# A graph network on one core: choosing the path without GpSimd, and three chunks gathered ahead

## The chip, the core and the metric

The kernel runs on one core of one Trainium2 chip. A core has a matrix engine (TensorE, PE in the profile, with its weight loads as PEld), VectorE (DVE), ScalarE (ACT), GpSimd (POOL) and SyncE (SP); all but VectorE and TensorE also issue transfers here, GpSimd the indirect ones that gather rows by an index. The metric is the time of one execution on the device, in microseconds; lower is better.

## The reference

A graph has N = 6250 nodes with 160 features each and E = 200,000 edges. Edges are sorted by destination. Two layers follow each other; each ends in a residual sum and a layer norm:

```python
# layer 0, per edge e: features of the source, weighted by the edge's four attributes
ss, vv = s[src], v[src]
m = concatenate([C0 * (ss*e0 @ W1 + dot(vv, e1)*INV3 @ W2), C1 * (p3 + p4 + p5)])
h = segment_sum(m, dst, num_segments=N) @ (Ws, Wv)
x1 = layernorm(2*x + relu(h))
# layer 1: an edge network gives weights w0..w3 of the messages
w = (relu(edge_attr_10 @ W_fc1) @ W_fc2)          # split into w0, w1, w2, w3
y = linear(x1)[src]                               # gathered by source again
out = layernorm(x1 + linear_si(x1) + 0.5 * o(segment_sums of w*y*e, dst))
```

What costs time is that 200,000 rows are gathered by `src` and summed by `dst`, in each of the two layers.

## The kernel before

Edges are cut into NCH = 391 chunks of 512: four edges on each of the 128 partitions. The host only lays arrays out: `src` and `dst` come as 128 x 391 x 4 integers. Since edges are sorted, the destinations of one chunk lie close together. For a chunk the kernel makes a one-hot matrix of (destination minus lowest destination of the chunk), at most 32 wide, scales it by the four edge attributes (`onehot`), and sums with it on TensorE (`matmuls`, L427); the result is transposed on VectorE (L447, L444) and added at a dynamic offset `low` to the accumulator `acc` (`add`, L449). The last 79 chunks (from HALF = 312) are treated as two half chunks, "windows", of 64 partitions each, so that there are NWIN = 470 windows.

This works only while no chunk spreads further than its width and no destination lies below what is closed already. So the kernel starts with a choice of path, in `gnn_kernel`: it computes the lowest and highest destination of every window, compares them with the constants `wide` and `closed`, and puts 1 or 0 into `fits`. Every engine loads `fits` and branches: `windowed` is the fast path, which runs here; `general` is the other one, which is never entered with these inputs.

The order in the choice of path before: constants by memsets on VectorE (L143); `src` on ScalarE's queue and `dst` on SP's; GpSimd makes `iota` (L154) and the identity matrix, then gathers chunk 0 (`gathered`, L206: four indirect transfers of 128 rows of 640 bytes). VectorE converts the destinations to floats (L159, `rel`), reduces over the four edges of each partition (L166, L167). GpSimd's all-reduce (L170) takes the maximum over partitions; the lowest enters it negated. Then GpSimd gathers chunk 1. VectorE evaluates the test on one partition (L175 to L190), and subtracts each window's lowest destination from `rel` (L193).

In `windowed`, VectorE first sets `eps` and `zero` (L229, L231). ScalarE clears `acc` with `zero` as its input (`clear`, L241, five pieces). The function `sums` issues the stages of a layer by hand, in steps t: `load` of chunk t, `onehot` of t-1, `matmuls` of t-2 and `add` of t-3 in layer 0; layer 1 adds `hidden` (L394, L397) and `message` (L407 to L415). Chunks 0 and 1 are in the tile `early`, the others go through a ring of GRING = 8 buffers `g`. At step 8 `prepare` builds the weights `wb` and `wn` of layer 0's end and `wc` of layer 1. When a block of 128 nodes is complete it goes through `projected` (with `wb`, L461), a layer norm, `linear` (with `wn`, L525), and is written to the table `ytab` from which layer 1 gathers.

In layer 1 the ten attributes of four chunks are loaded at a time into a tile `et` (L342). Two such tiles alternate: one is the memory of `early`, the other is a tile of its own from a pool `xp`. The order of the instructions on each engine is the order of the program here (`manual_schedule`), but for transfers, which the planner may put ahead on their queue.

Of the kernel before, what the change touches and what calls it, by code (L numbers as in the profile page):

```python
# [22 lines left out]
M0, M1 = 64, 32  # L23
J = 4
CH = P * J
NCH = -(-E // CH)
# [12 lines left out]
W = 32  # L39
NW = N + W + 2  # L40
HALF = 312
NWIN = HALF + 2 * (NCH - HALF)
WIDTHS = ((3, 32), (128, 16), (208, 24), (HALF, 32), (NCH, 24))
GRING = 8
PREPARE = 8


def expected(node, sign):
# [30 lines left out]
POS = {c: i for i, c in enumerate(ORDER)}  # L79
# [32 lines left out]
@with_exitstack  # L112
def gnn_kernel(ctx: ExitStack, tc: tile.TileContext, x, src, dst, ea, sh, avec,
               w1t, w2t, w3t, w4t, w5t, ws, wv, wsi0, wsi1, wl10, wl11,
               w00, w10, w01, w11, wfc1, wfc2, out):

    nc = tc.nc
    weights = (w1t, w2t, w3t, w4t, w5t, ws, wv, wsi0, wsi1, wl10, wl11, w00, w10, w01, w11, wfc1, wfc2)
    keep = ctx.enter_context(tc.tile_pool(name="keep", bufs=1))
    rel = keep.tile([P, NCH, J], F32, name="rel")
    srcs = keep.tile([P, NCH, J], I32, name="srcs")
    low = keep.tile([1, NWIN + 1], I32, name="low")  # L130
    fits = keep.tile([1, 1], I32, name="fits")
    ident = keep.tile([P, P], F32, name="ident")
    iota = keep.tile([P, W], F32, name="iota")
    early = keep.tile([P, 2, J, D], F32, name="early")
    ahead = {}
    with tc.manual_schedule(), tc.tile_pool(name="ends", bufs=1) as ep:
        dsts = ep.tile([P, NCH, J], I32, name="dsts")
        closed = ep.tile([1, NWIN], F32, name="closed")
        wide = ep.tile([1, NWIN], F32, name="wide")

        def fill(row, chunk, end, value):
            if chunk < end:
                nc.vector.memset(row[:, windows(chunk)[0]:windows(end - 1)[-1] + 1], float(value))  # L143

        begin = 0
        for c in range(1, NCH + 1):
            if c == NCH or floor_of(c) != floor_of(begin):
                fill(closed, begin, c, floor_of(begin))
                begin = c
        for (end, w), begin in zip(WIDTHS, (0,) + tuple(e for e, _ in WIDTHS)):  # L150
            fill(wide, begin, end, w)
        nc.scalar.dma_start(srcs, src)
        nc.sync.dma_start(dsts, dst)
        nc.gpsimd.iota(iota, pattern=[[1, W]], base=0, channel_multiplier=0,  # L154
                       allow_small_or_imprecise_dtypes=True)
        make_identity(nc, ident)

        ahead[0] = gathered(nc, early[:, 0], srcs, x, 0)
        nc.vector.tensor_copy(rel, dsts)  # L159

        mm = ep.tile([P, 2, NWIN], F32, name="mm")
        halves = [(slice(64 * h, 64 * h + 64), slice(HALF + h, NWIN, 2), slice(HALF, NCH)) for h in range(2)]
        parts = [(slice(0, P), slice(0, HALF), slice(0, HALF))] + halves
        nc.vector.memset(mm[:, :, HALF:NWIN], -2.0 * N)
        for rows, wins, chunks in parts:
            nc.vector.tensor_reduce(mm[rows, 0, wins], rel[rows, chunks, :], AX.X, ALU.max)  # L166
            nc.vector.tensor_reduce(mm[rows, 1, wins], rel[rows, chunks, :], AX.X, ALU.min)  # L167
            nc.vector.tensor_scalar(mm[rows, 1, wins], mm[rows, 1, wins], -1.0, None, op0=ALU.mult)
        mx = ep.tile([P, 2, NWIN], F32, name="mx")
        nc.gpsimd.partition_all_reduce(mx.rearrange("p a c -> p (a c)"), mm.rearrange("p a c -> p (a c)"),  # L170
                                       P, bass_isa.ReduceOp.max)
        ahead[1] = gathered(nc, early[:, 1], srcs, x, 1)
        nc.vector.memset(low, 0)
        lowf = ep.tile([1, NWIN], F32, name="lowf")
        nc.vector.tensor_scalar(lowf, mx[0:1, 1, :], -1.0, 0.0, op0=ALU.mult, op1=ALU.max)  # L175
        nc.vector.tensor_scalar(low[:, 0:NWIN], lowf, float(N), None, op0=ALU.min)
        far = ep.tile([1, 5], F32, name="far")
        span = ep.tile([1, NWIN], F32, name="span")
        nc.vector.tensor_add(span, mx[0:1, 0, :], mx[0:1, 1, :])
        nc.vector.tensor_sub(span, span, wide)  # L180
        nc.vector.tensor_reduce(far[:, 0:1], span, AX.X, ALU.max)
        for i, row in enumerate((mx[0:1, 0, 0:HALF], mx[0:1, 0, HALF:NWIN], mx[0:1, 1, :])):
            nc.vector.tensor_reduce(far[:, i + 1:i + 2], row, AX.X, ALU.max)
        nc.vector.tensor_add(closed, closed, mx[0:1, 1, :])
        nc.vector.tensor_reduce(far[:, 4:5], closed, AX.X, ALU.max)
        lim = ep.tile([1, 5], F32, name="lim")
        for i, v in enumerate((0, P * LATE, N + 1, 1, 1)):
            nc.vector.memset(lim[:, i:i + 1], float(v))
        nc.vector.tensor_tensor(far, far, lim, op=ALU.is_lt)
        nc.vector.tensor_reduce(fits, far, AX.X, ALU.min)  # L190
        for rows, wins, chunks in parts:
            n = chunks.stop - chunks.start
            nc.vector.tensor_tensor(rel[rows, chunks, :], rel[rows, chunks, :],  # L193
                                    mx[rows, 1, wins][:, :, None].to_broadcast([rows.stop - rows.start, n, J]),
                                    op=ALU.add)
    go = nc.values_load(fits[0:1, 0:1], min_val=0, max_val=1,
                        skip_runtime_bounds_check_because="a comparison's result")
    with tc.If(go > 0) as both:
        windowed(tc, x, srcs, rel, low, ident, iota, early, ahead, ea, sh, avec, *weights, out)
    with both.Else():  # L200
        general(tc, x, srcs, rel, dst, ea, sh, avec, *weights, out)


def gathered(nc, g, srcs, table, c):
    for j in range(J):
        nc.gpsimd.indirect_dma_start(out=g[:, j, :], out_offset=None, in_=table,  # L206
                                     in_offset=bass.IndirectOffsetOnAxis(ap=srcs[:, c, j:j + 1], axis=0))
    return g
# [3 lines left out]
def windowed(ctx: ExitStack, tc: tile.TileContext, x, srcs, rel, low, ident, iota, early, ahead, ea, sh, avec,  # L212
# [6 lines left out]
    nc = tc.nc  # L219
# [10 lines left out]
    zero = const.tile([P, 5], F32, name="zero")  # L230
    nc.vector.memset(zero, 0.0)  # L231
    a_sb = const.tile([P, NB], F32, name="a_sb")
    wb = const.tile([P, 5, D], F32, name="wb")
    wn = const.tile([P, 2 * D], F32, name="wn")
    wn2 = const.tile([M1, 2 * D], F32, name="wn2")
    wc = const.tile([P, 5, D], F32, name="wc")
    fc1 = const.tile([P, 100], F32, name="fc1")
# [74 lines left out]
    def sums(layer, table, gp, hp):  # L312
        with ExitStack() as s:
# [4 lines left out]
                up = s.enter_context(tc.tile_pool(name="up", bufs=1))  # L318
            pa = s.enter_context(tc.tile_pool(name=f"pa{layer}", bufs=3 if layer else 4, space=PSUM))
            if layer:  # L320
                xp = s.enter_context(tc.tile_pool(name="xp", bufs=1))
# [267 lines left out]
def general(ctx: ExitStack, tc: tile.TileContext, x, srcs, rel, dst, ea, sh, avec,  # L589
# [10 lines left out]
    nc = tc.nc  # L600
# [262 lines left out]
    with tc.tile_pool(name="any_acc0p", bufs=1) as ap0:  # L863
        acc = ap0.tile([P, NB, 4 * D], F32, name="acc0")
        sums(0, x, acc)
        with tc.tile_pool(name="any_n0", bufs=3) as np_, tc.tile_pool(name="any_n0t", bufs=1, space=PSUM) as pt, \
# [107 lines left out]
```

## Time and profile before

| what | value |
|---|---|
| median of three runs | 4930.06 us (4926.66 to 4936.89) |
| the profiled execution's own time | 4865.16 us |
| its span | 4863.0 us |
| PE, PEld busy | 2968.4 us (61%), 2222.4 us (46%) |
| DVE busy | 2162.4 us (44%) |
| ACT busy | 377.9 us (8%) |
| POOL busy | 2973.9 us (61%) |
| mean granted TensorE clock | 0.752 |
| layer 0, from the first ring gather to the last | 31.84 to 2248.4 us |
| first gather of layer 1 | 2291.78 us |

Times in the profile are microseconds from the start of the span. A row of the timeline gives start, duration, engine, line, operation, output and inputs, and in brackets how long the engine had been idle and what ended that. "remote" is an event that the profile can put down to no instruction of this core; "issue" is idle time in which the engine waited for nothing that the profile shows. A busy TensorE is not one at its peak, as its matmuls overlap and their ends are modelled.

### The profile page before, as it was taken

What the parts mean: (1) busy time and instruction counts of PE and PEld (TensorE: products, weight loads), DVE (VectorE), ACT (ScalarE), POOL (GpSimd) and SP (SyncE); (2) the same over time, 40 slices, a digit from 0 to 9 for tenths busy, and PEclk for the clock granted to TensorE, in tenths of its full rate; (3) what the DMA queues carried; (4) which work ended last, traced back from release to release, by engine and by line L of the source; (5) the groups of instructions that cost most, each with busy time, mean ns of one, the idle gap of its engine ahead of it and who ended that gap; (6) DMA issues with size and microseconds to landing.
All of it is one profiled execution on the core that took longest, in us unless ns stands there. A gap on an engine that the chain in (4) does not pass through costs nothing.

```text
span 4863.0 us, 42324 instructions
## 1 busy us (share of the span) xinstructions
PE 2968.4 (61%) x12714; PEld 2222.4 (46%) x12715; DVE 2162.4 (44%) x6948; ACT 377.9 (8%) x747; POOL 2973.9 (61%) x3137
## 2 busy tenths in 40 slices
PE   2333344444444444446587878777878788887777
PEld 1322333333333333434355555555555555555555
DVE  3222222232323333334355555555566566666656
ACT  2000000000000000001000000000100010101000
POOL 5666666666666666664665655565556656555553
PEclk7566655666666666667788888888888888888888
DMA  2222222222222222222222222222222222222221
GB/s 67 61 62 58 63 64 63 61 65 65 66 63 69 64 67 65 69 68 57 57 59 54 60 54 60 57 61 58 59 59 57 62 60 62 61 57 61 58 59 39
DMA packets 198246, 295.60 MB, mean 61 GB/s; under 512 B 59271, under 2 KB 140669, under 8 KB 198011
## 3 DMA queue, kind: packets, MB, share of 16 engines
q0 software_dynamic: 150144, 256.45, 21.4%
q1 hardware_dynamic: 40702, 31.55, 2.3%
q10 hardware_dynamic: 7164, 4.80, 0.3%
q8 instruction: 107, 1.75, 0.1%
q14 instruction: 129, 1.05, 0.1%
HBM read 280.57 MB, written 12.00 MB: 60 GB/s over the span
## 4 chain that ended last, share of the span: by engine, by line
PE 42%; another core or an unknown queue 33%; DVE 12%; issue 10%; POOL 2%; ACT 1%; DMA 0%; DVEq 0%; ACTq 0%; POOLq 0%
PE ab L427 24%; PE pw L407 11%; PE ph L394 3%; DVE m L415 3%; DVE S L385 2%; PE ph L461 2%; POOL g L206 2%; DVE acc L449 1%; PE bank L548 1%; DVE m L410 1%; DVE ab L444 1%; DVE ab L447 1%; DVE ab L445 1%; DVE bank L381 1%
## 5 line engine op out<-in xcount | busy, mean ns | idle before, releaser
L206 POOL DMA_INDIRECT g<-ytab,srcs x1564 | 1484.3, 949 | 1074.1 <-issue 438.5
L206 POOL DMA_INDIRECT g<-in_x,srcs x1556 | 1477.2, 949 | 741.8 <-issue 424.3
L427 PE MATMUL ab<-g,S 128*128 128x160 f32 (+1 forms) x3744 | 716.6, 392 | 818.6 <-issue 418.0
L427 PE MATMUL ab<-m,S 128*128 128x320 f32 (+1 forms) x3760 | 1087.9, 493 | 56.1 <-DVE acc L449 48.0
L427 PEld LDWEIGHTS ab<-g,S 128*128 128x128 f32 (+1 forms) x3744 | 638.5, 259 | 902.5 <-issue 441.2
L407 PE MATMUL pw<-fc,h 100*128 100x192 f32 x3128 | 737.3, 385 | 472.4 <-DVE m L415 375.1
L407 PEld LDWEIGHTS pw<-fc,h 100*128 100x128 f32 x3128 | 609.3, 222 | 703.1 <-issue 313.2
L427 PEld LDWEIGHTS ab<-m,S 128*128 128x128 f32 (+1 forms) x3760 | 698.3, 220 | 324.3 <-issue 161.9
L447 DVE STREAM_TRANSPOSE ab<-ab 128x160 f32<-128x160 f32 x470 | 169.6, 361 | 1232.0 <-remote 999.1
L385 DVE TENSOR_TENSOR S<-bank,sh 128x384 f32<-128x384 f32 (+2 forms) x782 | 431.5, 552 | 551.8 <-remote 189.8
L415 DVE TENSOR_TENSOR m<-g,pw 128x192 f32<-128x192 f32 x1564 | 475.9, 346 | 0.0
L410 DVE TENSOR_TENSOR m<-pw,g 128x256 f32<-128x256 f32 x782 | 328.1, 420 | 320.0 <-remote 208.9
L397 ACT ACTIVATE h<-ph 100x512 f32<-100x512 f32 x391 | 230.6, 597 | 2223.2 <-remote 983.1
L449 DVE TENSOR_TENSOR acc<-acc,ab 128x120 f32 (+2 forms) x940 | 261.7, 278 | 285.1 <-remote 176.3
L381 DVE TENSOR_TENSOR bank<-iota,rel 128x96 f32<-128x96 f32 (+2 forms) x782 | 200.2, 256 | 181.9 <-remote 96.9
L461 PE MATMUL ph<-wb,acc 128*128 128x160 f32 (+1 forms) x490 | 125.4, 430 | 246.9 <-DVE acc L449 107.2
L461 PEld LDWEIGHTS ph<-wb,acc 128*128 128x128 f32 (+1 forms) x490 | 109.6, 286 | 264.3 <-issue 117.1
L445 DVE STREAM_TRANSPOSE ab<-ab 32x160 f32<-32x160 f32 x470 | 165.5, 352 | 16.2
L444 DVE STREAM_TRANSPOSE ab<-ab 128x160 f32<-128x160 f32 x470 | 167.4, 356 | 10.7 <-issue 6.7
L394 PE MATMUL ph<-early,fc 10*100 10x512 f32 x392 | 114.9, 648 | 0.3
L394 PE MATMUL ph<-et,fc 10*100 10x512 f32 x390 | 112.0, 642 | 0.2 <-issue 0.2
L525 PE MATMUL pl<-wn,xT 128*128 128x320 f32 (+1 forms) x98 | 49.4, 593 | 87.1 <-issue 60.2
(80 smaller groups left out, 732.3 us busy)
## 6 DMA issues: line engine op xcount, KB each, us to landing
g<-ytab,srcs POOLq DMA_INDIRECT x1564
g<-in_x,srcs POOLq DMA_INDIRECT x1556
raw<-in_sh SPq DMA_DIRECT2D x88, 64.0 KB
early<-in_ea SPq DMA_DIRECT2D x98, 40.0 KB
xt<-in_x SPq DMA_DIRECT2D x48, 80.0 KB
ytab<-y ACTq DMA_DIRECT2D x48, 80.0 KB
btab<-base SPq DMA_DIRECT2D x48, 80.0 KB
et<-in_ea SPq DMA_DIRECT2D x96, 40.0 KB
```

What stands on the lines that cost most here:

```text
L206: nc.gpsimd.indirect_dma_start(out=g[:, j, :], out_offset=None, in_=table, in_offset=bass.IndirectOffsetOnAxis(ap=srcs[:, c, j:j + 1], axi ...
L381: nc.vector.tensor_tensor(oh[:, :, :w], iota[:, None, :w].to_broadcast([P, J, w]), rel[:, c, :, None].to_broadcast([P, J, w]), op=ALU.is_e ...
L385: nc.vector.tensor_tensor(S[c][:, :, :, :w], oh[:, :, None, :w].to_broadcast([P, J, 4, w]), attr[:, :, :, None].to_broadcast([P, J, 4, w]) ...
L394: nc.tensor.matmul(ph[:, i, :], fc1[g:g + 10, :], ET[c // 4][g:g + 10, c % 4 // 2, :], start=True, stop=True)
L397: nc.scalar.activation(H[c], H["p"][:, c % 2, :].rearrange("f (p j) -> f j p", j=J), AF.Relu, scale=FC_SCALE)
L407: nc.tensor.matmul(pw[:, j, :], h[:, q + j, :], fc2, start=True, stop=True)
L410: nc.vector.tensor_tensor(mq[:, :, :, 0:64], pw[:, :, 0:128].rearrange("p j (a u) -> p j a u", a=2), y[:, :, None, 0:64].to_broadcast([P, ...
L415: nc.vector.tensor_tensor(mq[:, :, a, 64:160].rearrange("p j (d u) -> p j d u", d=3), y1, pw[:, :, None, w:w + 32].to_broadcast([P, 2, 3, ...
L427: nc.tensor.matmul(ab[:, :n], one[h * i:h * i + h, j, :, :], t[h * i:h * i + h, j, :], start=(j == 0), stop=(j == J - 1), skip_group_check ...
L447: nc.vector.transpose(tr, blocks[:, 0])
L449: nc.vector.tensor_tensor(v, v, tr[:, :, :width(c)], op=ALU.add)
L461: nc.tensor.matmul(po[:r], lhs, weights[:, g, :], start=(g == 0), stop=(g == 4))
```

## The change

- `ramp`, 0 to 127 along each row, is made by VectorE with seven doublings, and `iota` becomes its first 32 columns. `ident` is a comparison of `ramp` with each partition's own number. GpSimd makes neither.
- The indices of the first three chunks come in a small transfer of their own, `first`; all three chunks are gathered into `early`, which grows from two chunks to three, ahead of the choice. `dst` goes to ScalarE's queue, `src` to SP's behind `first`.
- `wide` and `closed` are brought onto partitions, one window per row and five columns ("folds": three of 104 chunks, and the two halves of the last 79), by ten matmuls with a one.
- Highest and lowest of each partition are reduced over all 391 chunks, transposed on TensorE (four transpositions each), and reduced along the row on VectorE. The all-reduce goes.
- The test works on 104 partitions and five columns; failures are counted by one matmul with ones.
- The lowest is brought back to all partitions by five matmuls with the identity (`lows`, in PSUM), and subtracted from `rel`. `low` is now made last.
- In layer 1 the second attribute tile is no longer in a pool of its own: it shares the memory of `wb` and `wn` (`w_or_et`).

```diff
+AHEAD = 3
+FOLD = 104
...
-    iota = keep.tile([P, W], F32, name="iota")
-    early = keep.tile([P, 2, J, D], F32, name="early")
+    ramp = keep.tile([P, P], F32, name="ramp")
+    iota = ramp[:, 0:W]
+    early = keep.tile([P, AHEAD, J, D], F32, name="early")
...
+        first = ep.tile([P, AHEAD, J], I32, name="first")
+        nc.sync.dma_start(first, src[:, 0:AHEAD, :])
+        nc.scalar.dma_start(dsts, dst)
+        nc.sync.dma_start(srcs, src)
+        for i in range(AHEAD):
+            ahead[i] = gathered(nc, early[:, i], first, x, i)
+        nc.vector.memset(ramp[:, 0:1], 0.0)
+        for k in range(7):
+            nc.vector.tensor_scalar(ramp[:, 1 << k:2 << k], ramp[:, 0:1 << k], float(1 << k), None, op0=ALU.add)
+        own = ep.tile([P, 32], F32, name="own")
+        nc.vector.transpose(own, ramp[:, 0:32])
+        for b in range(1, 4):
+            nc.vector.tensor_scalar(own[32 * b:32 * b + 32, 0:1], own[32 * b:32 * b + 32, 0:1], float(32 * b), None,
+                                    op0=ALU.add)
+        nc.vector.tensor_scalar(ident, ramp, own[:, 0:1], None, op0=ALU.is_equal)
...
-        nc.scalar.dma_start(srcs, src)
-        nc.sync.dma_start(dsts, dst)
-        nc.gpsimd.iota(iota, pattern=[[1, W]], base=0, channel_multiplier=0,
-                       allow_small_or_imprecise_dtypes=True)
-        make_identity(nc, ident)
-        ahead[0] = gathered(nc, early[:, 0], srcs, x, 0)
+        late = NCH - HALF
+        folds = [(k, FOLD, slice(FOLD * k, FOLD * k + FOLD)) for k in range(3)]
+        folds += [(3 + h, late, slice(HALF + h, NWIN, 2)) for h in range(2)]
...
+        for a, row in enumerate((wide, closed)):
+            for k, n, wins in folds:
+                nc.tensor.matmul(consts[0:n, a, k:k + 1], row[0:1, wins], ones[0:1, 0:1], start=True, stop=True)
+        nc.vector.tensor_copy(bounds[:, :, 0:3], consts[:, :, 0:3])
+        nc.vector.tensor_copy(bounds[0:late, :, 3:5], consts[0:late, :, 3:5])
         nc.vector.tensor_copy(rel, dsts)
+        for a, op in enumerate((ALU.max, ALU.min)):
+            nc.vector.tensor_reduce(mm[:, a, :], rel, AX.X, op)
+            tp = pp.tile([FOLD, 4, P], F32, name=f"tp{a}")
+            for k in range(4):
+                n = FOLD if k < 3 else late
+                nc.tensor.transpose(tp[0:n, k, :], mm[:, a, FOLD * k:FOLD * k + n], ident)
+            nc.vector.tensor_reduce(ends[:, a, 0:3], tp[:, 0:3, :], AX.X, op)
+            nc.vector.tensor_reduce(ends[0:late, a, 3:5], tp[0:late, 3, :].rearrange("p (h e) -> p h e", h=2), AX.X, op)
...
+        nc.tensor.matmul(count, ones[0:FOLD, :], bad.rearrange("p a k -> p (a k)"), start=True, stop=True)
+        nc.vector.tensor_reduce(total, count, AX.X, ALU.add)
+        nc.vector.tensor_scalar(fits, total, 0.5, None, op0=ALU.is_lt)
+        lows = pp.tile([P, NWIN], F32, name="lows")
+        for k, n, wins in folds:
+            nc.tensor.matmul(lows[:, wins], ends[0:n, 1, k:k + 1].to_broadcast([n, P]), ident[0:n, 0:n],
+                             start=True, stop=True)
...
-        nc.gpsimd.partition_all_reduce(mx.rearrange("p a c -> p (a c)"), mm.rearrange("p a c -> p (a c)"),
-                                       P, bass_isa.ReduceOp.max)
-        ahead[1] = gathered(nc, early[:, 1], srcs, x, 1)
...
-                                    mx[rows, 1, wins][:, :, None].to_broadcast([rows.stop - rows.start, n, J]),
-                                    op=ALU.add)
+                                    lows[rows, wins][:, :, None].to_broadcast([rows.stop - rows.start, n, J]),
+                                    op=ALU.subtract)
+        nc.vector.memset(low, 0)
+        nc.vector.tensor_scalar(low[:, 0:NWIN], lows[0:1, :], 0.0, float(N), op0=ALU.max, op1=ALU.min)
...
-    wb = const.tile([P, 5, D], F32, name="wb")
-    wn = const.tile([P, 2 * D], F32, name="wn")
+    w_or_et = const.tile([P, 7 * D], F32, name="w_or_et")
+    wb = w_or_et[:, :5 * D].rearrange("p (g d) -> p g d", d=D)
+    wn = w_or_et[:, 5 * D:]
...
-                    if POS[c] % 8 >= 4:
-                        et = xp.tile([P, 2, CH], F32, name="et")
-                    else:
-                        et = early.rearrange("p a j d -> p (a j d)")
-                        et = et[:, :2 * CH].rearrange("p (s e) -> p s e", s=2)
+                    et = w_or_et if POS[c] % 8 >= 4 else early.rearrange("p a j d -> p (a j d)")
+                    et = et[:, :2 * CH].rearrange("p (s e) -> p s e", s=2)
```

In `general`, one pool of work tiles goes from three buffers to two; that path is not entered.

More of the change, by code (lines that the diff above doesn't have):

```diff
@@ L132, in gnn_kernel @@
     ident = keep.tile([P, P], F32, name="ident")
-    iota = keep.tile([P, W], F32, name="iota")
-    early = keep.tile([P, 2, J, D], F32, name="early")
+    ramp = keep.tile([P, P], F32, name="ramp")
+    iota = ramp[:, 0:W]
+    early = keep.tile([P, AHEAD, J, D], F32, name="early")
     ahead = {}
-    with tc.manual_schedule(), tc.tile_pool(name="ends", bufs=1) as ep:
+    with tc.manual_schedule(), tc.tile_pool(name="ends", bufs=1) as ep, \
+            tc.tile_pool(name="folds", bufs=1, space=PSUM) as pp:
         dsts = ep.tile([P, NCH, J], I32, name="dsts")
@@ L151, in gnn_kernel @@
             fill(wide, begin, end, w)
-        nc.scalar.dma_start(srcs, src)
-        nc.sync.dma_start(dsts, dst)
-        nc.gpsimd.iota(iota, pattern=[[1, W]], base=0, channel_multiplier=0,
-                       allow_small_or_imprecise_dtypes=True)
-        make_identity(nc, ident)
-        ahead[0] = gathered(nc, early[:, 0], srcs, x, 0)
-        nc.vector.tensor_copy(rel, dsts)
-        mm = ep.tile([P, 2, NWIN], F32, name="mm")
+        ones = ep.tile([P, 1], F32, name="ones")
+        nc.vector.memset(ones, 1.0)
@@ new lines, in gnn_kernel @@
+        late = NCH - HALF
+        folds = [(k, FOLD, slice(FOLD * k, FOLD * k + FOLD)) for k in range(3)]
+        folds += [(3 + h, late, slice(HALF + h, NWIN, 2)) for h in range(2)]
+        consts = pp.tile([FOLD, 2, 5], F32, name="consts")
+        bounds = ep.tile([FOLD, 2, 5], F32, name="bounds")
+        ends = ep.tile([FOLD, 2, 5], F32, name="ends")
+        nc.vector.memset(bounds[:, 0, :], 1.0)
+        nc.vector.memset(bounds[:, 1, :], 0.0)
+        nc.vector.memset(ends, 0.0)
+        for a, row in enumerate((wide, closed)):
+            for k, n, wins in folds:
+                nc.tensor.matmul(consts[0:n, a, k:k + 1], row[0:1, wins], ones[0:1, 0:1], start=True, stop=True)
@@ new lines, in gnn_kernel @@
+        nc.vector.tensor_copy(bounds[:, :, 0:3], consts[:, :, 0:3])
+        nc.vector.tensor_copy(bounds[0:late, :, 3:5], consts[0:late, :, 3:5])
+        nc.vector.tensor_copy(rel, dsts)
+        mm = ep.tile([P, 2, NCH], F32, name="mm")
+        for a, op in enumerate((ALU.max, ALU.min)):
[6 more added lines that the diff above has]
+            nc.vector.tensor_reduce(ends[0:late, a, 3:5], tp[0:late, 3, :].rearrange("p (h e) -> p h e", h=2), AX.X, op)
@@ new lines, in gnn_kernel @@
+        bad = ep.tile([FOLD, 4, 5], F32, name="bad")
+        nc.vector.tensor_sub(bad[:, 0, :], ends[:, 0, :], ends[:, 1, :])
+        nc.vector.tensor_tensor(bad[:, 0, :], bad[:, 0, :], bounds[:, 0, :], op=ALU.is_ge)
+        nc.vector.tensor_scalar(bad[:, 1, 0:3], ends[:, 0, 0:3], float(P * LATE), None, op0=ALU.is_ge)
+        nc.vector.tensor_scalar(bad[:, 1, 3:5], ends[:, 0, 3:5], float(N + 1), None, op0=ALU.is_ge)
+        nc.vector.tensor_scalar(bad[:, 2, :], ends[:, 1, :], 0.0, None, op0=ALU.is_lt)
@@ new lines, in gnn_kernel @@
+        nc.vector.tensor_tensor(bad[:, 3, :], ends[:, 1, :], bounds[:, 1, :], op=ALU.is_lt)
+        count = pp.tile([1, 20], F32, name="count")
+        nc.tensor.matmul(count, ones[0:FOLD, :], bad.rearrange("p a k -> p (a k)"), start=True, stop=True)
+        total = ep.tile([1, 1], F32, name="total")
+        nc.vector.tensor_reduce(total, count, AX.X, ALU.add)
[4 more added lines that the diff above has]
+                             start=True, stop=True)
@@ L162, in gnn_kernel @@
         halves = [(slice(64 * h, 64 * h + 64), slice(HALF + h, NWIN, 2), slice(HALF, NCH)) for h in range(2)]
         parts = [(slice(0, P), slice(0, HALF), slice(0, HALF))] + halves
[L164 to L168, printed above, removed]
@@ L169, in gnn_kernel @@
-        mx = ep.tile([P, 2, NWIN], F32, name="mx")
-        nc.gpsimd.partition_all_reduce(mx.rearrange("p a c -> p (a c)"), mm.rearrange("p a c -> p (a c)"),
-                                       P, bass_isa.ReduceOp.max)
-        ahead[1] = gathered(nc, early[:, 1], srcs, x, 1)
[L173 to L190, printed above, removed]
         for rows, wins, chunks in parts:
@@ L320, in sums @@
             if layer:
-                xp = s.enter_context(tc.tile_pool(name="xp", bufs=1))
                 ph_ = s.enter_context(tc.tile_pool(name="ph", bufs=1, space=PSUM))
@@ L865, in general @@
         sums(0, x, acc)
-        with tc.tile_pool(name="any_n0", bufs=3) as np_, tc.tile_pool(name="any_n0t", bufs=1, space=PSUM) as pt, \
+        with tc.tile_pool(name="any_n0", bufs=2) as np_, tc.tile_pool(name="any_n0t", bufs=1, space=PSUM) as pt, \
                 tc.tile_pool(name="any_n0m", bufs=2, space=PSUM) as pm:
```

## The prediction

> **What bounds the kernel now.** I read the page first, then the timeline of the first 100 us, the waits, and the stretches. The page says that no engine is full and that a third of the chain hangs on something the profile cannot name:
>
> ```profile
> PE 2968.4 (61%) x12714; PEld 2222.4 (46%) x12715; DVE 2162.4 (44%) x6948; ACT 377.9 (8%) x747; POOL 2973.9 (61%) x3137
> ...
> PE 42%; another core or an unknown queue 33%; DVE 12%; issue 10%; POOL 2%; ACT 1%; DMA 0%; DVEq 0%; ACTq 0%; POOLq 0%
> ```
>
> The change touches the first 33 us, so the timeline there decides what can be won:
>
> ```profile
> 7.37 0.97 DVE L159 CAST rel<-dsts 128x1564 f32<-128x1564 int32 x1 [4.60 <-DMA dsts<-in_dst]
> ...
> 10.02 0.16 POOL L154 IOTA iota<- 128x32 f32 x1 [9.56 <-issue]
> ...
> 21.91 3.04 POOL L170 PARTITION_ALL_REDUCE mx<-mm  x1 [5.94 <-issue]
> 24.98 0.39 DVE L175 TENSOR_SCALAR lowf<-mx 1x470 f32<-1x470 f32 x1 [10.52 <-POOL mx L170]
> ...
> 30.34 0.15 DVE L190 TENSOR_REDUCE fits<-far 1x1 int32<-1x5 f32 x1
> 30.41 2.33 DVE L193 TENSOR_TENSOR rel<-rel,mx 128x1248 f32<-128x1248 f32 x3
> ...
> 32.82 0.06 DVE L231 MEMSET zero<- 128x5 f32 x1
> 32.96 1.28 ACT L241 ACT_TABLE_LOAD   x1 [32.83 <-DVE zero L231]
> ...
> 34.25 26.75 ACT L241 ACTIVATE acc<-zero 128x6284 f32<-128x6284 f32 x5
> ```
>
> See: VectorE sits 10.52 us behind POOL's all-reduce, of which 5.94 us is POOL getting ready for it. `fits` stands at 30.49, `zero` at 32.88. Then comes the link that matters: ScalarE can clear `acc` only after `zero`, and takes 26.75 us, to 61.00. What comes after:
>
> ```profile
> 61.04 0.32 DVE L449 TENSOR_TENSOR acc<-acc,ab 128x160 f32 x1 [21.52 <-issue]
> ...
> 81.97 0.37 DVE L447 STREAM_TRANSPOSE ab<-ab 128x160 f32<-128x160 f32 x1 [16.17 <-remote]
> ```
>
> And POOL in the same timeline:
>
> ```profile
> 94.11 0.95 POOL L206 DMA_INDIRECT g<-in_x,srcs  x1 [7.15 <-remote]
> ```
>
> The first addition into `acc` stood 21.52 us ready and started 40 ns after the last clear. So the pipeline of layer 0 really starts at 61.0, and whatever moves `zero` moves that start. After it VectorE waits for PE (L447 waits for PE alone, by the program) and POOL, which gathers every 1.25 us (0.95 + 0.30), comes to a stop at 87 with its ring of eight buffers full. From there POOL follows the matmuls: the 1556 gathers of layer 0 into the ring would take 1556 x 1.253 = 1950 us and took 2217 (31.84 to 2249). Why PE's results come so late after its records end is not shown; I only need that the stretch is paced from there, not by POOL.
>
> **The change, part by part.** Sums are made in the profiled execution: span 4863.0, its own time 4865.2 us; the runs' median is 4930.1, 64.9 us more, which no row explains. I carry the difference in us to the median. A move of under 0.2% (9.9 us) cannot be told from no change in this kernel's measurement.
>
> *VectorE ahead of the cast.* Begins at 0.83 as before. `ramp` has one memset and seven doublings that wait for each other: nearest row 0.19 (the 32-wide tensor_scalar, L275) plus 0.04 of semaphore, 7 x 0.23 + 0.06 = 1.7. Transpose, three small adds and the 128x128 comparison (0.30 as L381's 128x128): 0.15 + 0.3 + 0.3. `closed` and `wide` as now, 1.38 + 0.59. Four memsets 0.25. Sum 0.83 + 4.7 = 5.5. Then ten one-column matmuls on PE turn `wide` and `closed`: at 0.2 each (L261's pair of 32-column passes took 0.31; one column moves less) 2.0, from `wide` ready at 5.2, so 7.2, and two copies 0.4: 7.7. Bounds: 0.05 and 0.31 each give 6.1 and 8.8. The destinations landed at 7.37; they have ScalarE's queue now and the 0.8 MB of `srcs` starts about 0.4 (one issue) later beside them, so I keep 7.4. The cast begins at 7.7 (7.4 to 9.0), 0.3 later than now.
>
> *Ends of the chunks.* Cast 0.97. Each reduction now takes 1564 columns: 1.39 x 1564/1248 = 1.74. Four transpositions follow, L511's mean 0.37 each, 1.5, and 0.1 of release; the columns come back through a reduction of 384 and one of 128 per row, 0.57 and 0.2 by L166's 0.47 for 316. VectorE does these in order, with no second reduction to cover the transpositions: 1.74 + 1.6 + 0.8 = 4.1 for the highest, 4.1 for the lowest. So 7.7 + 0.97 + 8.2 = 16.9. What it replaces: L164 to L168 (8.36 to 13.85) and the wait for POOL to 24.98, 16.6 us against 8.2.
>
> *Test.* Six operations of five columns at 0.15 (L189) 0.95, the count's matmul 0.5, two more operations 0.35: `fits` at 18.7, against 30.49. Before, twelve rows of 0.39 to 0.64 on one partition (24.98 to 30.49, 5.5 us); now 1.8.
>
> *Lowest back to all partitions.* Five matmuls behind the count's: L427 took 2 x 0.267 between starts for 160 columns at half clock, so 0.35 for 104; 1.6 and 0.3 of latency from 18.3: 20.2. If each takes as long as the slowest of VectorE's waits for a chunk suggests (4 matmuls in 5.6 us, 1.4 each) it is 25.3; the first is the likelier, since the first chunk's four matmuls were out within 2.5 us of 36.63. The subtraction costs 2.33 as L193 does: 22.5. `low`'s memset and its one remaining operation now stand ahead of `zero`: 0.45 + 0.45. `zero` at 23.5, against 32.82: **9.3 us earlier**. With the bounds above, 28.6 to 22.
>
> *A new wait.* `eps` and `zero` wait for all twelve early gathers to land (the memory of the small index tile is reused), and so do ScalarE's table load and SP's `a_sb` with every weight transfer queued behind it. The twelfth starts 1.30 + 0.30 + 10 x 1.25 = 14.1 after the first and takes 0.95; for landing I take 1.7, as `raw`'s transfers were issued by 32.88 and let VectorE go at 34.57. `first` is 128 pieces of 48 bytes on SP's queue, beside the 0.8 MB of destinations: it lands between 2.9 (issue by 1.16, and 1.7) and, behind them, 7.4; I take 4.5. The last gather then lands at 4.5 + 14.1 + 2.65 = 21.3: hidden by 2.2 us. If `first` comes with the destinations, 24.2, and 0.7 is lost. Here a rule of the Trainium skill speaks against the change: SBUF — State Buffer, "Who interferes with whom", says that a cast or tensor_scalar of VectorE in its two-port mode locks GpSimd out for the whole instruction, so descriptor generation stands still. The row: beside L168's 0.32 us tensor_scalar the next gather took 0.96 as ever, and the one at 26.74 took 1.12. By the row the gathers lose nothing; by the rule, the cast's 0.97 and the doublings' 1.5, an estimate of 2.5 us, and the last landing is 23.8, and 0.3 is lost. I take the row.
>
> *POOL.* It loses iota, identity and all-reduce, and gathers three chunks, not two, before the choice. It goes on at max(18.7 + 1.35, 19.9) = 20.1 after 12 gathers; before at 31.84 after 8: 31.84 + 4 x 1.25 - 20.1 = 16.8 us ahead. That is worth nothing while the ring is full at the first stall.
>
> *Layer 1's attribute tile.* It shares memory with `wb` and `wn`, so SP's first transfer into it waits for the last `linear` of layer 0. Before, it was issued at 2109; now about 2288. It is used at 2308.5 (L394), 20 us later; `raw`'s 64 KB needed 1.7 to land. Behind it in SP's queue stand the last `btab` row, which waited until 2288 anyway, and `early<-in_ea`, which went out at 2298. Cost 0; uncovered, each us past 20 costs one. Inside layer 1 the two tiles alternate as before, and no instruction changes its place on PE, ACT or DVE.
>
> Sum: -9.3 us, all at the start. 4865.2 becomes 4855.9; 4930.1 becomes **4920.8**.
>
> **Rivals.**
> *Gathers set layer 0.* If outside the profiled execution POOL, at 1.253 us each, is never stopped by the ring, the 16.8 us count: 4913. For it: 1950 of 2217 us are POOL's own. Against: 249 us of its waits end at "remote" and it stopped already at 87.
> *POOL starts late.* The change frees POOL of 9.56 us of "issue" ahead of the iota. If that belongs to POOL's start and not to the iota, the gathers begin at 10.2, the last lands at 27.0, and `zero` follows at 27.1: only 5.7 us, 4924. Against: the same kind of wait (5.94) came back before the all-reduce only.
> *Slower: the clock of layer 0.* The start moves against PE's activity windows:
>
> ```profile
> 100.00:500.00 400.00, 132.94 (x690) 119.65 (x690) 97.91 (x330) 4.23 (x9) 264.65 (x281) 0.61 0.24 60
> 500.00:2248.00 1748.00, 766.27 (x3613) 641.16 (x3614) 530.87 (x1613) 89.81 (x253) 1164.85 (x1227) 0.64 0.26 65
> 2292.00:4863.00 2571.00, 2019.08 (x8156) 1424.43 (x8156) 1479.12 (x4793) 243.86 (x440) 1484.12 (x1564) 0.85 0.23 58
> ```
>
> (Stretch, length, busy PE, weight load, DVE, ACT, POOL, then granted clock.) In layer 0 the mean is about 0.63. A hundredth of clock less is 1.6% of some 2150 us, 34 us. It decides from a mean 0.0055 lower: 19 us, the 9.3 and 9.9 more. At 0.01 the time is 4955. For it: the profiled execution lies 65 us off the runs with the same code. Against: the three runs lie within 10.2 us of each other.
>
> **How the numbers follow.** The start moves by 9.3, give or take 4: 0.46 (of it 0.20 beyond 9.9). Gathers set layer 0: 0.22. POOL starts late: 0.14. Clock lower, slower: 0.13. Clock higher, below 4905: 0.05. Faster 0.20 + 0.22 + 0.05 = 0.47; same 0.26 + 0.14 = 0.40; slower 0.13. The likeliest is 4921, by itself 4916 to 4925. The range leaves out the higher clock and most of the lower: 4902 to 4940.
>
> **What would show it.** In the profile after: the cast at 7.4 to 9; `fits` at 18 to 20; POOL's first gather by 6 and no all-reduce; `zero` near 23.5 and the clears ended near 51.7; the first addition right behind; layer 1's first gather near 2282 instead of 2291.8; `w_or_et`'s transfer landed well before its matmul. Wrong would make it: the first gather at 10, `lows` matmuls of over 1 us, or a layer 0 whose length differs by more than 5 us from now.

## The result

The changed kernel takes 4911.0 us (median; 4906.6 to 4923.8) beside 4929.0 us (4923.4 to 4941.5) for the kernel before on the same chip: a ratio of 0.9969, interval 0.9952 to 0.9986, so **18 us faster** (7 to 24). Predicted were 4921, between 4902 and 4940, with faster as the likeliest of the three signs. The number held. The reason given for it did not hold on two other chips, where the runs below were made: there it is not the start of the clears that counts but the start of the gathers. On this chip the cause of the 18 us stays open.

### The profile after

The page of the changed kernel, busy time of the engines and the chain that ended last. Its span is 4916.5 us and its own time 4918.2; the profiled execution of before had 4865.2, some 65 us under its own median, so that these two executions can't be subtracted from each other as wholes.

```profile
PE 2987.0 (61%) x12754; PEld 2237.0 (46%) x12755; DVE 2157.6 (44%) x6955; ACT 376.2 (8%) x747; POOL 2961.3 (60%) x3133
...
PE 37%; another core or an unknown queue 36%; DVE 13%; issue 11%; POOL 2%; ACT 1%; DMA 0%; DVEq 0%; ACTq 0%; POOLq 0%
```

As a whole nothing has moved. The timeline of its first 70 us:

```profile
5.79 1.08 POOL L241 DMA_INDIRECT early<-in_x,first  x1 [5.30 <-DMA first<-in_src]
...
8.42 1.23 POOL L241 DMA_INDIRECT early<-in_x,first  x1 [0.30 <-issue]
8.50 0.15 DVE L191 COPY bounds<-consts 79x4 f32<-79x4 f32 x1
8.57 0.96 DVE L194 CAST rel<-dsts 128x1564 f32<-128x1564 int32 x1
...
17.81 2.42 PE L220 MATMUL lows<-ident,ends 104*128 104x104 f32 x10
...
18.11 0.14 DVE L216 TENSOR_SCALAR fits<-total 1x1 int32<-1x1 f32 x1
...
21.23 0.95 POOL L241 DMA_INDIRECT g<-in_x,srcs  x1 [0.30 <-issue]
...
22.92 2.34 DVE L226 TENSOR_TENSOR rel<-rel,lows 128x1248 f32<-128x1248 f32 x3 [4.67 <-remote]
...
27.10 0.06 DVE L266 MEMSET zero<- 128x5 f32 x1
...
28.53 26.75 ACT L278 ACTIVATE acc<-zero 128x6284 f32<-128x6284 f32 x5
...
55.31 0.32 DVE L482 TENSOR_TENSOR acc<-acc,ab 128x160 f32 x1 [10.05 <-issue]
...
68.50 0.94 POOL L241 DMA_INDIRECT g<-in_x,srcs  x1 [7.58 <-PE ab L460]
```

See: all-reduce and iota are gone, POOL starts at 5.79 and goes from early gathers to ring gathers at 21.23 without a pause. `fits` stands at 18.25. But `zero` is made at 27.10, only 5.7 us earlier than before (32.82), because the subtraction got `lows` only at 22.92, though by the records its matmuls were over at 20.23: again a wait of VectorE that ends at "remote", as at 81.97 in the kernel before. The clears end at 55.28 instead of 61.0.

Follow the gathers by their number. In the kernel before, the 9th is the first into the ring; the 13th, the 53rd, the 100th and the last of layer 0 are:

```profile
37.13 0.95 POOL L206 DMA_INDIRECT g<-in_x,srcs  x1 [0.30 <-issue]
...
94.11 0.95 POOL L206 DMA_INDIRECT g<-in_x,srcs  x1 [7.15 <-remote]
...
164.61 0.94 POOL L206 DMA_INDIRECT g<-in_x,srcs  x1 [0.30 <-issue]
...
2248.40 0.94 POOL L206 DMA_INDIRECT g<-in_x,srcs  x1 [0.30 <-issue]
```

The same four of the kernel after (its 13th, at 21.23, is shown above), and its first one of layer 1:

```profile
78.50 0.95 POOL L241 DMA_INDIRECT g<-in_x,srcs  x1 [0.30 <-issue]
...
146.34 0.94 POOL L241 DMA_INDIRECT g<-in_x,srcs  x1 [0.30 <-DMA g<-in_x,srcs]
...
2245.68 0.95 POOL L241 DMA_INDIRECT g<-in_x,srcs  x1 [0.30 <-issue]
...
2289.74 0.94 POOL L241 DMA_INDIRECT g<-ytab,srcs  x1 [43.10 <-DMA w_or_et<-in_ea]
```

The lead is 37.13 - 21.23 = 15.9 us at the 13th, and 15.6 at the 53rd. In between the changed kernel stands still once for 7.58 us (at 68.50), and the kernel before once for 7.15 (at 94.11): a full ring costs each about the same. At the 100th it is 18.3 us. So up to here the gathers lead by far more than the first addition, which came 5.7 us earlier (61.04 and 55.31). Then the lead melts, to 2.7 us at the end of layer 0, and layer 1 of this execution is 55 us longer than that of before (4916.5 - 2289.7 against 4863.0 - 2291.8). The medians differ by 18 us the other way, so most of that is probably a difference between two executions; what makes it isn't shown. A lower clock in layer 0 is one candidate: between 500 and 2248 us the granted clock is 0.64 in the profile before and 0.63 in this one, and at the price set in the prediction, 34 us for a hundredth, half a hundredth would be 17 us. What the lead is worth at the end can't be read from this pair, and was tried by experiment.

### The profile page after: what moved, and what is told of

Same layout as the page of the kernel before. It is cut to its first block, busy times and chain, and to the rows that moved or that the text cites. A ratio compares the mean times of both kernels' runs of the same rounds, so it can differ in the third digit from the quotient of the medians.

```text
span 4916.5 us, 42451 instructions
## 1 busy us (share of the span) xinstructions
PE 2987.0 (61%) x12754; PEld 2237.0 (46%) x12755; DVE 2157.6 (44%) x6955; ACT 376.2 (8%) x747; POOL 2961.3 (60%) x3133
## 4 chain that ended last, share of the span: by engine, by line
PE 37%; another core or an unknown queue 36%; DVE 13%; issue 11%; POOL 2%; ACT 1%; DMA 0%; DVEq 0%; ACTq 0%; POOLq 0%
PE ab L460 21%; PE pw L440 9%; DVE m L448 3%; DVE S L418 3%; PE ph L427 2%; POOL g L241 2%; PE ph L494 2%; DVE m L443 1%; DVE acc L482 1%; PE bank L581 1%; DVE ab L477 1%; DVE ab L478 1%; DVE bank L414 1%; DVE ab L480 1%
## 5 line engine op out<-in xcount | busy, mean ns | idle before, releaser
L460 PE MATMUL ab<-g,S 128*128 128x160 f32 (+1 forms) x3736 | 739.3, 401 | 967.8 <-issue 593.8
L460 PEld LDWEIGHTS ab<-g,S 128*128 128x128 f32 (+1 forms) x3736 | 655.8, 266 | 1055.3 <-issue 585.3
L414 DVE TENSOR_TENSOR bank<-ramp,rel 128x96 f32<-128x96 f32 (+2 forms) x782 | 199.3, 255 | 192.3 <-remote 99.7
L494 PE MATMUL ph<-w_or_et,acc 128*128 128x160 f32 (+1 forms) x490 | 119.5, 414 | 208.4 <-DVE acc L482 102.0
L494 PEld LDWEIGHTS ph<-w_or_et,acc 128*128 128x128 f32 (+1 forms) x490 | 105.2, 275 | 224.1 <-issue 102.3
L427 PE MATMUL ph<-w_or_et,fc 10*100 10x512 f32 x390 | 114.5, 645 | 2.3 <-issue 1.9
L530 ACT ACTIVATE rl<-ph 128x160 f32<-128x160 f32 (+1 forms) x49 | 14.8, 302 | 1078.4 <-remote 805.1
```

The costliest lines, as they stand in the source:

```text
L414: nc.vector.tensor_tensor(oh[:, :, :w], iota[:, None, :w].to_broadcast([P, J, w]), rel[:, c, :, None].to_broadcast([P, J, w]), op=ALU.is_e ...
L427: nc.tensor.matmul(ph[:, i, :], fc1[g:g + 10, :], ET[c // 4][g:g + 10, c % 4 // 2, :], start=True, stop=True)
L460: nc.tensor.matmul(ab[:, :n], one[h * i:h * i + h, j, :, :], t[h * i:h * i + h, j, :], start=(j == 0), stop=(j == J - 1), skip_group_check ...
L494: nc.tensor.matmul(po[:r], lhs, weights[:, g, :], start=(g == 0), stop=(g == 4))
```

## The experiments

Two theories. **Clears** (the one predicted with): layer 0 begins when ScalarE's clears let the first addition through; what moves `zero` moves the end. **Gathers** (the rival *Gathers set layer 0*): POOL's row of 3128 indirect transfers sets the length of the kernel, and only its start and its pauses count.

These kernels ran on two other chips: the unedited kernel before, POOL kept waiting, clears at the start and two chunks ahead on one, the rest on the other. On both the kernel before takes 3980 to 3981 us instead of 4929, and its profile looks different; so it was profiled there, unchanged.

> The kernel before, unchanged, as a measure of the measurement. All theories: ratio 1, its interval within 0.2% of it. Its profile is wanted too: if the profiled execution of before that the forecast used was an unusual one, this span lies near the median of the runs (about 4925) and not at 4863, and the place where the 60 us come back is layer 1 (2292 us onward), since layer 0 of the kernel after ended within 3 us of before's.

Measured: 3981.1 us, ratio 1.0001 (0.9993 to 1.0009). (The other question of this run, why the profiled execution of before was 65 us under its median, stays open, as it fell on another chip.) Its page, busy time and chain, then its waits of POOL (total, number, longest), then its 13th gather and its first addition:

```profile
PE 3256.2 (82%) x12714; PEld 2151.5 (54%) x12715; DVE 2187.1 (55%) x6948; ACT 380.5 (10%) x747; POOL 2968.2 (75%) x3137
...
POOL 28%; issue 22%; DMA 20%; PE 18%; DVE 10%; ACT 1%; DVEq 0%; ACTq 0%; POOLq 0%
```

```profile
POOL g L206 <- issue: 806.7, 2643, 1.5
POOL g L206 <- PE ab L427: 61.0, 200, 0.3
...
POOL g L206 <- DMA ytab<-y: 22.4, 1, 22.4
```

```profile
37.72 0.94 POOL L206 DMA_INDIRECT g<-in_x,srcs  x1 [0.30 <-issue]
...
61.63 0.32 DVE L449 TENSOR_TENSOR acc<-acc,ab 128x160 f32 x1 [21.51 <-ACT acc L241]
```

"Unknown queue" is gone from the chain, POOL leads it, and no wait of a ring gather but the one between the layers is longer than 1.5 us: 3128 gathers of 0.947 + 0.30 us are 3900 of 3982 us. The waits put down to PE are the same 0.30 us that stand before any gather. On the first chip the profile puts 383.6 us of POOL's waits down to VectorE's one-hots (L381) and 249.4 to "remote" in before, and 390.3 and 271.5 in after. The names are inferred, and by the program a one-hot frees no buffer of the ring; but that POOL stood still there is plain.

### The change itself, and what it is made of

*The changed kernel, unedited.*

> The changed kernel, nothing edited, beside the four that are compared here. If POOL's gathers set the length of layer 0: the first ring gather starts at 21.2 to 21.4 instead of 31.8, with twelve gathers behind it instead of eight, 16.5 us ahead: -16.5 us (-15 to -18). If the end of ScalarE's clears sets it: -5.7 us, the 61.0 to 55.3 of the profile.

Measured: 3964.6 us against 3980.8, ratio 0.9959 (0.9945 to 0.9973): **-16.3 us**. Its timeline on this chip:

```profile
20.25 2.34 DVE L226 TENSOR_TENSOR rel<-rel,lows 128x1248 f32<-128x1248 f32 x3 [2.01 <-PE lows L220]
...
20.64 0.94 POOL L241 DMA_INDIRECT g<-in_x,srcs  x1 [0.30 <-issue]
...
24.44 0.06 DVE L266 MEMSET zero<- 128x5 f32 x1
...
52.65 0.32 DVE L482 TENSOR_TENSOR acc<-acc,ab 128x160 f32 x1 [23.12 <-ACT acc L278]
```

Here `lows` came at 20.25, the first addition stands 9.0 us earlier than in before (61.63), and the 13th gather about 17 us earlier (37.3 to 37.7 in the runs whose start is that of before). So the two theories are 8 us apart, 9.0 against 17, and 16.3 was measured.

*POOL kept waiting, nothing else.* The changed kernel with memsets on POOL between early and ring gathers:

```diff
+    idle = keep.tile([P, 128], F32, name="idle")
...
         nc.vector.tensor_scalar(low[:, 0:NWIN], lows[0:1, :], 0.0, float(N), op0=ALU.max, op1=ALU.min)
+        for _ in range(64):
+            nc.gpsimd.memset(idle, 0.0)
```

> The changed kernel with about 53 small memsets on POOL between the twelfth early gather and the branch, some 13 us at 0.25 each; nothing else waits for them. If the start of layer 0 is set by the clears of the accumulator (the forecast's theory), POOL still fills its ring before PE asks for it: as fast as the changed kernel, 18 us under before. If gathers set layer 0 (the rival), POOL's head start of 15.6 us is the gain, and most of it goes: some 5 us under before.

Measured: 3979.6 us, ratio 0.9998 (0.9989 to 1.0006). Its timeline:

```profile
20.92 13.88 POOL L233 MEMSET idle<- 128x128 f32 x53
...
25.86 26.75 ACT L281 ACTIVATE acc<-zero 128x6284 f32<-128x6284 f32 x5
35.99 0.95 POOL L244 DMA_INDIRECT g<-in_x,srcs  x1 [1.19 <-issue]
```

The clears are as early as in the changed kernel, the 13th gather is back to within 1.7 us of before, and **the whole gain is gone**: 0.8 us are left, where the theory of the gathers had expected some 5. The memsets and the wait behind them put that gather off by some 15 us, not by 13. (Eleven of the memsets were put behind POOL's last gather, where nothing waits for them.)

*Clears at the start.* The opposite: `acc` and `zero` in the memory that both paths share, the five clears issued at once.

```diff
+    acc = keep.tile([P, 5, NW], F32, name="acc")
+    zero = keep.tile([P, 5], F32, name="zero")
...
         nc.scalar.dma_start(dsts, dst)
+        nc.vector.memset(zero, 0.0)
+        for k in range(5):
+            nc.scalar.activation(acc[:, k, :], zero[:, 0:1].to_broadcast([P, NW]), AF.Copy)
...
-                if not layer:
-                    for k in range(2 * t, min(2 * t + 2, 5)):
-                        clear(k)
```

> The changed kernel with the accumulator kept outside the fast path and cleared by ScalarE from the first microsecond, beside the choice of path, so that the clears end near 30 us and not at 55.3. Theory of the clears: the first addition is at about 38 instead of 55.3 (two chunks of one-hot and matmuls after zero), 17 to 25 us faster than the changed kernel, 35 to 43 under before. Theory of the gathers: layer 0 is no shorter than POOL's pace, so no more than 3 us over the changed kernel's gain.

Measured: 3962.6 us, ratio 0.9956 (0.9942 to 0.9969). The timeline:

```profile
2.50 26.75 ACT L156 ACTIVATE acc<-zero 128x6284 f32<-128x6284 f32 x5
...
21.25 0.95 POOL L246 DMA_INDIRECT g<-in_x,srcs  x1 [0.30 <-issue]
...
29.64 0.32 DVE L481 TENSOR_TENSOR acc<-acc,ab 128x160 f32 x1
```

The first addition is 32 us earlier than before and nothing of it arrives: -17.8 us with a lead of 16.5 in the gathers. Against the changed kernel (16.3 us, measured on the other chip) that is no gain that can be told.

*Fewer chunks ahead.* First two chunks, with the attribute tile of layer 1 in a pool of its own again; then one chunk.

```diff
-AHEAD = 3
+AHEAD = 2
...
+                xp = s.enter_context(tc.tile_pool(name="xp", bufs=1))
```

> The changed kernel with two chunks gathered ahead instead of three, and with layer 1's second attribute tile in memory of its own again; the choice of path is the new one. If only the start counts: as the changed kernel, 18 us under before. If gathers set layer 0: 5 us less gain (four gathers at 1.25), 13 under before. If the shared tile was what won or lost time at the change of layers, the first gather of layer 1 and the time of layer 1 differ from the changed kernel's by more than 5 us.

```diff
-        for i in range(AHEAD):
+        for i in range(1):
             ahead[i] = gathered(nc, early[:, i], first, x, i)
```

> The new choice of path, but only chunk 0 is gathered ahead of it. Gathers: the first ring gather stays near 19.7, as in the run with two chunks ahead, but has four gathers behind it instead of twelve: the thirteenth gather at 19.7 + 8 x 1.25 = 29.7, 8.2 us ahead of the kernel before and 8.4 behind the changed one: -8 us against before. Clears: VectorE's zero no longer waits for early gathers, the clears end at about 52.6 as with two chunks ahead, 2.7 us sooner than in the changed kernel: -8.4 us against before, and faster than the changed kernel by 2.7. What tells them apart is the difference to the changed kernel: +8.4 or -2.7.

Measured: with two chunks 3967.2 us, ratio 0.9968 (0.9956 to 0.9981), -13.2; with one 3974.4 us, 0.9985 (0.9978 to 0.9991), -6.4. In both the clears are as early as in the changed kernel (first addition at 52.64 and 52.44). The timeline with one chunk, the first gather after the branch, which is its fifth, and its 13th:

```profile
19.58 0.94 POOL L241 DMA_INDIRECT g<-in_x,srcs  x1 [9.26 <-issue]
...
29.58 0.95 POOL L241 DMA_INDIRECT g<-in_x,srcs  x1 [0.30 <-issue]
```

Its 13th stands at 29.58, 8 us ahead of before; with two chunks the 13th stands at 24.65, 13.1 ahead. With one chunk ahead the clears theory expected more than the changed kernel's gain; it was 9.8 us less. As for the shared attribute tile: layer 1's first gather came after an idle time of 22.63 us with a tile of its own, 22.93 with the shared one and 22.36 in before.

### More work for ScalarE

The kernel before with the first clear done twice, and, without the condition on `k`, with all five done twice:

```diff
                     for k in range(2 * t, min(2 * t + 2, 5)):
                         clear(k)
+                        if not k:
+                            clear(k)
```

> The kernel before, with the first of ScalarE's five clears done twice: 5.35 us more of ScalarE ahead of the first addition, which moves from 61 to 66.4; no gather is moved. Clears: +5.3 us. Gathers: 0 within 1.5 us, since the eight buffers are full only at 71.8 and the first of them is freed before that.

> The kernel before, with each of the five clears done twice: 26.75 us more of ScalarE, the first addition at about 88 instead of 61. Clears: +26.7 us. Gathers: only what POOL stands still counts. Its ring fills at 71.8; chunk 2's one-hot stands ahead of the first addition on VectorE and frees one buffer, chunk 3's stands behind it, so POOL stops from about 77 to 90: +13 us (10 to 18).

Measured: one more clear 3980.7 us beside 3980.5, ratio 1.0001 (0.9993 to 1.0010); five more 3995.5, ratio 1.0039 (1.0025 to 1.0052), **+15.1 us**. The timelines, first with one more clear, then with five:

```profile
67.10 0.32 DVE L449 TENSOR_TENSOR acc<-acc,ab 128x160 f32 x1 [27.02 <-ACT acc L241]
...
72.71 0.95 POOL L206 DMA_INDIRECT g<-in_x,srcs  x1 [0.30 <-PE ab L427]
```

```profile
34.43 54.10 ACT L241 ACTIVATE acc<-zero 128x6284 f32<-128x6284 f32 x10
88.56 0.32 DVE L449 TENSOR_TENSOR acc<-acc,ab 128x160 f32 x1 [48.94 <-ACT acc L241]
...
92.32 0.94 POOL L206 DMA_INDIRECT g<-in_x,srcs  x1 [15.31 <-PE ab L427]
```

Five and a half microseconds more before the first addition cost nothing. Twenty-seven cost what POOL stood still: 15.31 less its usual 0.30 is 15.0, and 15.1 was measured. That settles how the clears enter on this chip: through the ring's eight buffers.

### A delay that didn't take

Memsets on VectorE ahead of `eps` and `zero`, in the kernel before and in the changed one (`nc.vector.memset(idle, 0.0)`, 64 times, placed as POOL's were).

> The kernel before with 64 memsets of 128 x 128 on VectorE between the subtraction and eps and zero, 5 to 9 us at 0.08 to 0.14 each; no gather is moved. Clears: the clears and the first addition come 5 to 9 us later, so +5 to +9 us. Gathers: nothing, within 1 us, as long as POOL finds a free buffer: its eight are full at 31.84 + 40 = 71.8, and chunk 2's matmuls free one before that.

> The changed kernel with the same 64 memsets of VectorE ahead of eps and zero, 5 to 9 us. Clears: the whole 5 to 9 us are lost against the changed kernel. Gathers: the ring is full at 21.3 + 40 = 61.3, and the first addition, at 60 to 64 now, holds chunk 3's one-hot behind it, whose matmuls free the first buffer some 5 us later; so POOL stops once, for 4 to 8 us, and about that much of the 16.5 is lost. The two theories price this one alike; it is to show where the clears begin to count: a stop of POOL at 61, and its length equal to the loss.

Measured: 3996.4 us, ratio 1.0039 (1.0025 to 1.0053), and 3978.7, ratio 0.9993 (0.9985 to 1.0001): +15.6 against before, and +14.2 against the changed kernel. It looks as if the clears counted, and more than was expected; but the timeline of the first of them shows another kernel than the one meant (the second shows the same, 63 memsets from 3960.11 on):

```profile
33.21 0.17 DVE L198 MEMSET idle<- 128x128 f32 x1
33.33 0.06 DVE L234 MEMSET zero<- 128x5 f32 x1
...
3977.54 16.18 DVE L198 MEMSET idle<- 128x128 f32 x63 [2.71 <-issue]
```

One memset stayed in its place and 63 were put at the end of VectorE's work, behind the last layer norm, where they take 16.18 us and the kernel became 15.6 us longer. `zero` stands where it was (33.33). The runs say nothing of the two theories; doubling the clears took their place.

### A faster start

Indices first: the destinations on SP's queue behind the small transfer instead of beside it, alone and with the clears at the start.

```diff
         nc.sync.dma_start(first, src[:, 0:AHEAD, :])
-        nc.scalar.dma_start(dsts, dst)
+        nc.sync.dma_start(dsts, dst)
```

> The changed kernel with the destinations on SP's queue behind the small transfer of indices, instead of on ScalarE's beside it. Gathers: first lands alone, the first gather starts near 3.5 instead of 5.1 to 5.8, twelve gathers end 2 us sooner, and the first ring gather follows the branch at 19.7 instead of 20.7 to 21.3: -1 to -1.6 us against the changed kernel, -17.5 against before. Clears: nothing beyond what zero moves, under 0.5 us, as zero stands behind lows and not behind the gathers. If the first transfer's time is its own and not its neighbour's, nothing moves.

> The same with acc and zero moved to the memory that both paths share and the five clears issued at the start, so that they end before 30. Gathers: as with the indices alone, -17.5 us against before; where POOL stopped once at 60 for 7.6 us, as in the profile of the changed kernel, that stop goes as well and the gain is up to 25. Clears: the first addition moves from 61 to about 30, -30 us.

Measured: 3965.2 us, ratio 0.9962 (0.9948 to 0.9975), and 3963.1, ratio 0.9955 (0.9941 to 0.9969), beside -16.3 us for the changed kernel. The timeline of the first:

```profile
2.89 1.08 POOL L241 DMA_INDIRECT early<-in_x,first  x1 [2.41 <-DMA first<-in_src]
...
8.03 1.61 POOL L241 DMA_INDIRECT early<-in_x,first  x1 [0.30 <-issue]
8.56 0.96 DVE L194 CAST rel<-dsts 128x1564 f32<-128x1564 int32 x1
...
19.67 0.94 POOL L241 DMA_INDIRECT g<-in_x,srcs  x1 [1.25 <-issue]
```

The transfer did land 2.25 us earlier without its neighbour (2.89 against 5.14), but POOL then waited 1.25 us for the branch, and 1.0 us of lead was left. A gain of that size can't be told here: -15.3 and -17.4 lie on either side of -16.3. No version was found that beats the changed kernel by more than 1.5 us.

### The runs side by side

Lead of the 13th gather and of the first addition over the kernel before, from the timelines (before: for the runs on the chip of *before_again* its 37.72, for the others 37.5, as the three runs there that begin like before have 37.3 to 37.7; and 61.6), and the measured gain, all in us:

| kernel | gathers' lead | first addition's lead | gain |
|---|---|---|---|
| changed kernel | 16.9 | 9.0 | 16.3 |
| two chunks ahead | 13.1 | 9.0 | 13.2 |
| one chunk ahead | 7.9 | 9.2 | 6.4 |
| POOL kept waiting | 1.7 | 9.0 | 0.8 |
| clears at the start | 16.5 | 32.0 | 17.8 |
| indices first | 17.8 | 9.0 | 15.3 |
| indices first, clears at the start | 17.7 | 31.9 | 17.4 |
| one more clear | -0.2 | -5.5 | -0.2 |
| five more clears | 0.2, then -14.8 with the stop | -26.9 | -15.1 |

The gain follows the first column to within 2.5 us and doesn't follow the second.

## Why the prediction was right, and where it was not

The time fell in the range, and faster was called. Luck has a share in that: the change moves the gathers and the clears the same way, by 17 and 9 us on the other chips, so that a sum over the wrong one had the right sign. By its own steps:

- **What bounds the kernel: the step that failed.** "So the pipeline of layer 0 really starts at 61.0, and whatever moves `zero` moves that start." The row was read rightly: the addition does start 40 ns after the last clear. But it is not what is late next. POOL's gathers run on meanwhile, and on the other chips the addition held them up only when the ring was full. There one more clear moved the addition by 5.5 us and the time by nothing, and clears at the start moved it by 32 us and the time by 17.8, about the gathers' lead of 16.5.
- **"That is worth nothing while the ring is full at the first stall": wrong.** On the first chip the ring did fill, in both kernels, and behind the first long stop of each the lead was 15.6 us, as it had been ahead of them (15.9). I had added up what POOL's stop takes away in the kernel before and not asked whether the changed one would have the same.
- **The rival that came true on the other chips** is *Gathers set layer 0*: 16.8 us by its sum, 4913 us. Measured were 16.3 there and 18 on the first, 4911. I gave it 0.22, because in the profile before POOL waits for PE from 87 on. That is a fact of the first chip, and there it stays open how much of the 18 us is the gathers' lead: the interval, 7 to 24 us, holds 9.3 as well as 16.8, and none of the experiments ran there. Two of the prediction's own signs went against it on the first chip: layer 0, from the first ring gather to the last, took 2224 us against 2217, 8 us longer where at most 5 were allowed, and the first gather of layer 1 came at 2289.7, not near 2282.
- **The choice of path, by its parts.** Right: first gather at 5.8 ("by 6"), no all-reduce, the first ring gather at 21.23 (predicted 20.1, as `first` was expected at 4.5) instead of 31.84. `fits` at 18.25 (predicted 18.7) is right because errors cancel: the cast began at 8.57 and not at 7.7, as the ten one-column matmuls took 3.3 us (5.08 to 8.38) and not 2.0; cast and ends took 8.35 us and not 9.2, the test 1.3 and not 1.8. Mis-sized on the first chip: `lows` came back at 22.92 and not 20.2, and `zero` at 27.10, not 23.5. By the records the matmuls were over at 20.23, as the sum had it (2.42 us of them, not 1.6, but begun at 17.81); that VectorE gets such a result late, here by 2.7 us, I had read in the same profile; a later time for it, 25.3, I had weighed and put aside. Another 0.9 us came behind it: `low`'s operation took 0.64 us and not 0.45, and VectorE stood idle for 0.54 ahead of `eps`. On the other chip `lows` came at 20.25 and `zero` at 24.44.
- **POOL starts late** (5.7 us): its cause was wrong. The 9.56 us ahead of the iota belonged to the iota; without it POOL began as soon as `first` landed, at 5.79, and with the indices first at 2.89. That `zero` came 5.7 us earlier on the first chip, as in that rival, has another reason, `lows`.
- **The attribute tile: right.** A tile of its own and the shared one differ by 0.3 us at layer 1's first gather.
- **VectorE and POOL side by side.** I took the row, no loss, and read it at the wrong gather. The 0.32 us of L168 lie inside the gather ahead of the one that I looked at, and it took 1.30 us, where the first gather of the changed kernel took 1.08. So the row didn't speak for no loss:

```profile
10.90 1.30 POOL L206 DMA_INDIRECT early<-in_x,srcs  x1 [0.20 <-issue]
11.38 0.32 DVE L168 TENSOR_SCALAR mm<-mm 128x312 f32<-128x312 f32 x1
...
12.50 0.96 POOL L206 DMA_INDIRECT early<-in_x,srcs  x1 [0.30 <-issue]
```

  In the changed kernel the gather beside the cast took 1.23 us, 1.28 to 1.61 in its variants, and 0.95 otherwise: the cast cost it 0.3 to 0.7 us. More telling is where it ended. In all six runs in which it had begun ahead of the cast it ended 0.12 us after the cast did (9.65 and 9.53 here, 9.64 and 9.52 with the indices first), however early it had begun; in the three in which it began inside the cast, it ended 0.81 to 0.82 us after. So as to the end these runs agree with the Trainium skill, SBUF — State Buffer, "Who interferes with whom", by which GpSimd is locked out for the whole of such an instruction: no gather ended before the cast beside it did. But not all of a gather stood still meanwhile. In the changed kernel only 0.15 us ahead of the cast and 0.12 us behind it, of the 0.95 that a gather takes, lay outside it, so the loss is less than the cast's whole 0.96 us. It is small beside the 16 us.
- **The clock** did nothing that could be seen on the other chips: means of 0.779 with the change, and 0.78 without. On the first, 0.750 and 0.752, it can't be ruled out as a part of the difference (see the profile after).

## What to carry to other kernels

A link of the chain, "B starts when A ends", is worth its time only if what sets the end waits for B. Where a stage is fed by a long row of equal operations through a ring of buffers, find out whether that row ever stands still; if not, its first operation and its pauses are the kernel's time, and everything beside it has as much slack as the ring has buffers. And look whether an operation put in for a delay is where it was put: at the end of an engine's work it shows up as a cost of its own.

## What was not expected of the hardware

- **One chip is not another.** The same kernel takes 4929 us on the first chip and 3980 on two others. The clock alone doesn't explain it: the mean granted clock was 0.752 on the first and 0.78 there, and between 500 and 1900 us it was even higher on the first, 0.63 against 0.58, though layer 0 took 2217 us on the first and 1947 on another. (In layer 1 it was lower on the first, 0.85 against 0.98, and may have a part there.) What the profiles show to differ is that PE's results come late on the first chip: `lows` reached VectorE 2.7 us after the recorded end of its matmuls on the first chip, and 0.04 us after it on the other (2.42 us of matmuls on both), and a third of the first chip's chain is "another core or an unknown queue", and none of it on the others. What delays them isn't shown, nor that this is the whole of the difference.
- **A small transfer beside a large one.** 128 pieces of 48 bytes let POOL go at 2.89 us with the 0.8 MB of destinations behind them on their own queue, and at 5.06 to 5.79 with the destinations issued at the same moment on another queue.
- **Iota and all-reduce of GpSimd** were preceded by 9.6 to 10.1 and 5.9 to 6.2 us in which POOL waited for nothing that the profile shows; the operations themselves took 0.16 and 3.04.
